# Loads that write all 128 partitions at once in place of loads that write 32 partitions with four pieces each, in a fused attention and mixture-of-experts kernel

## The chip, the cores and the metric

The kernel runs on one core of one Trainium2 chip. The metric is the device time of one execution in microseconds (us), as the median of several runs. A core has five engines, each with its own in-order instruction queue: TensorE (PE, matrix multiplies), VectorE (DVE), ScalarE (ACT), GpSimd (POOL) and SyncE (SP, which here does nothing but issue DMAs). The DMAs are executed by 16 DMA engines, which all queues share. The on-chip memory SBUF has 128 partitions; DRAM is the off-chip memory.

## The reference

Four batches of 512 tokens (width 512) go through two layers, all in float32:

```
h = layernorm(x)
q = feature_map(h @ Wq.T);  gate = sigmoid(h @ Wg.T + bg)
k, v = split(ctx @ Wkv.T);  k = feature_map(k)          # 1024 context rows, 16 heads of 32
attn = (q @ (k.T @ v)) / (q @ sum(k))                    # linear attention
x = x + (attn * gate) @ Wo.T
h2 = layernorm(x)
w, sel = top_2(h2 @ Wr);  w = softmax(w)                 # 2 of 8 experts per token
x = x + sum over the 2 experts e of w_e * (h2 @ We[e] + be[e])
```

## The kernel before, in words

**The order of the work.** PE executes its matmuls in an order written out by hand. Per batch there are eight steps over the context, `kv_tiles` (line 374; per step the products `pk` and `pv` of one 128-row tile `cT`, and `kvs`), then the query and gate projections `pq` and `pg`, the products `pz` and `pn`, and the output projection `po`. The context steps of the next batch are laid between the stages of the present one: steps 0 to 3 ahead of `po`, steps 4 to 7 behind it.

**Routing and experts.** After `po`, the router (`choose`, line 526) makes the transposes `pt`, the logits `ps` and `pl`, and the top two; `dispatch` (line 580) counts places with small matmuls `pp` and writes each token's normalized row twice, by indirect DMA from the POOL queue, into `stream`, a DRAM buffer with a region for each expert. A row is 514 floats: 512 of the token and two numbers. The buffer is first filled with empty rows (`stream<-empty`, 1 MB each, from SP). The expert tiles of 128 rows are then run by `run` (line 738): 17 early tiles of the first three batches' tokens, whose loads begin once the third batch is counted, and 18 late tiles, whose list is known only after the last batch's `dispatch`. For each tile:

- `rows` (line 742) loads the tile from `stream` into `xg` with four DMAs of 64 KB, and two numbers a row into `of`. It runs five tiles ahead of the matmuls, on five buffers.
- `turned` (line 776) transposes 32x32 blocks on DVE, three tiles ahead of the matmuls.
- `expert` (line 796) multiplies with the weights `we_sb` of the tile's expert (`pe`), and DVE adds the bias into `y`.
- POOL writes `y` by indirect DMA to `result`, a DRAM buffer with two rows a token. Later the rows are fetched back (`fetch`, line 871), added with their gates (`add`, line 896) and stored (`store`, line 911), in part between the late tiles and in part at the end.

**A layout of the weights.** A DVE transpose turns 32x32 blocks, so a token's 512 features lie in SBUF with feature 128 i + 32 c + f at partition 32 i + f of chunk c. The weights that multiply such operands, `wq`, `wg` and the eight experts' `we`, are loaded in the same layout: `load_rows` (line 132) for `wg_in` and `wq_sb` (lines 167, 173), and the loop in `kv_tiles` (line 382) for `we_sb`. Each does it with four DMAs of 256 KB; DMA i writes the 32 partitions 32 i to 32 i + 31, with four pieces of 2 KB for each. The loads `xg` do it in the same way, with four pieces of 512 bytes for each of 32 partitions. The query blocks `blocks` (`load_blocks`, line 112) are loaded with 32 partitions and sixteen pieces each.

**What sets the order around the change.** SP's queue is in order, and all of these loads are on it: first `wkv`, three `cT` tiles and four `x` tiles, then `wg_in`, `cT` tile 3, `wq_sb`, `blocks`, `wr_in`, `cT` tile 4, and the loads of `wo` and `bg`. A `cT` tile has three buffers, so that tile s + 2 is loaded when tile s - 1 has been used. The experts' weights are loaded in the second and third batches, one expert at every second context step, behind that step's `cT` load and ahead of its `stream<-empty`. SP's and ACT's DMAs share eight semaphores in turn, and each DMA waits for the one eight places before it to land. Matmuls of SP-loaded tiles wait for the semaphore of the load. DVE's, ACT's and POOL's orders are chosen by a list scheduler when the program is built.

Of the kernel before, what the change touches and what calls it, by code (L numbers as in the profile page):

```python
# [17 lines left out]
P = 128  # L18
B, L, S, D = 4, 512, 1024, 512
E, F = 8, 512  # L20
HD = 32
NC = D // P
# [31 lines left out]
def xattn_moe_kernel(  # L54
# [47 lines left out]
    def load(dst, src):  # L102
        latest["load"] = nc.sync.dma_start(out=dst, in_=src)  # L103
        tc.keep_in_program_order(latest["load"])

    def load_ctx(b, s):
        t = cpool.tile([P, ROW], F32, tag="cT", name=f"cT_{b}_{s}")
        t = t[:, 0:D].rearrange("p (c n) -> p c n", n=P)
        load(t, cT[b, s])
        return t  # L110
# [21 lines left out]
    def load_rows(dst, w):  # L132


        for i in range(NC):
            load(dst[ts(i, HD)], w.rearrange("(c f) i n -> i f c n", f=HD)[i])

    wkv_sb = wpool.tile([P, NC, 2 * D], F32, tag="wkv", name="wkv_sb")
    wq_sb = wpool.tile([P, NC, D], F32, tag="wq", name="wq_sb")
# [3 lines left out]
    nc.gpsimd.memset(wr_sb, 0.0)  # L143
    bg_sb = wpool.tile([P, NC], F32, name="bg_sb")
    we_sb = wpool.tile([P, E, NC, F], F32, name="we_sb")
    we_rows = we.rearrange("e (c f) i n -> e i f c n", f=HD)

    ctx_tiles = {}

# [172 lines left out]
    def keys(b, s):  # L322
        k = kvpool.tile([P, D], F32, tag="k", name=f"k_{b}_{s}")
        feature_map(k, half_tile(ctx_tiles[b, s], 0, "pk"))
        return k
# [27 lines left out]
    def set_empty(b, e):  # L353
        r = e * CAP + b * L
        n = L if b < B - 1 else CAP - b * L
        set_rows(r, n)
        if (b, e) == (B - 1, E - 1):
            set_rows(SLOTS, P)
            load(
                result[NOWHERE:, :].rearrange("(r p) f -> p r f", p=P),  # L360
                empty[:, 0:F].rearrange("p (o f) -> p o f", o=1).to_broadcast([P, 2 * NT, F]),
            )
# [11 lines left out]
    def kv_tiles(b, lo, hi, between=None, inside=None):  # L374
        for s in range(lo, hi):
            nxt = (b, s + 2) if s + 2 < NS else (b + 1, s + 2 - NS)
            if nxt[0] < B and nxt not in loaded_ctx:
                loaded_ctx.add(nxt)
                ctx_tiles[nxt] = load_ctx(*nxt)
            if b in (1, 2) and s % 2 == 0:  # L380
                e = (b - 1) * E // 2 + s // 2
                for i in range(NC):
                    load(we_sb[ts(i, HD), e], we_rows[e, i])
            for e in (s,) if b else (2 * (s - NS // 2), 2 * (s - NS // 2) + 1):
                if e >= 0:
                    set_empty(b, e)
            if s == 0:
                sums[b] = pkv.tile([P, NC, 2 * P], F32, tag="kvs", name="kvs")
            k = made.pop(s) if s in made else keys(b, s)
            if (b, s) == (0, 0):  # L390
                made[1] = keys(0, 1)
            if inside is not None and s == lo:
                inside()
            v = values(b, s)
            if s > 0:
                kv_add(sums[b], s - 1, *pending[b])
            pending[b] = k, v
            if between is not None:
                between(s - lo)
        if hi == NS:  # L400
            kv_add(sums[b], NS - 1, *pending[b])
# [336 lines left out]
    def run(lists, lo, n, early):  # L738
        why = "clamped to the tiles of the streams and to the experts where it is computed"
        no_i, row_i, ranked = lists  # L740

        def rows(j):


            row = nc.values_load(
                row_i[0:1, j : j + 1], [ET.SP], min_val=0, max_val=SLOTS,
                skip_runtime_bounds_check_because=why,
            )
            if (j if early else j + EARLY) % 5 < 3:
                xg = cpool.tile([P, ROW], F32, tag="cT", name="xg")  # L750
            else:
                xg = kvpool.tile([P, ROW], F32, tag="v", name="xg", bufs=2)
            of = small.tile([P, 2], F32, tag="of", name="of", bufs=8)
            rows_of = stream[ds(row, P), :]
            parts = []
            for i in range(NC):
                parts.append(
                    (
                        xg[ts(i, HD), 0:D].rearrange("t (j f) -> t j f", j=NC),
                        rows_of[:, ts(i, P)].rearrange("(j t) f -> t j f", t=HD),  # L760
                    )
                )
            parts.append((of, rows_of[:, D:ROW]))
            for dst, src in parts:
                load = nc.sync.dma_start(out=dst, in_=src)  # L765
                latest["load"] = load
                if early:
                    behind(load, written["stream"][: 2 * NT * (B - 1)], "tokens of the tile")
                    early_loads.append(load)
                    for put in scatters.get(B - 1, []):  # L770
                        tc.declare_no_dep(load.ins, put.ins, reason=full_already)
                else:
                    behind(load, written["stream"], "tokens of the tile")
            return xg, of

        def turned(j, xg, of):

            if early:
                xT = turned_rows[:, j % 4]
            else:  # L780
                xT = work.tile([P, NC, P], F32, tag="qT", name="xgT", bufs=NC)
            latest["turn"] = nc.vector.transpose(  # L782
                xT.rearrange("p c (j t) -> p j c t", t=HD),
                xg[:, 0:D].rearrange("p (j c f) -> p j c f", j=NC, f=HD),
            )

            home_i = small.tile([P, 1], U32, tag="to", name="to", bufs=8)
            tc.keep_in_program_order(latest["turn"])
            latest["turn"] = nc.vector.tensor_scalar(
                home_i, of[:, 1:2], ranked[:, j : j + 1], of[:, 0:1],  # L790
                ALU.is_equal, ALU.add,
            )
            tc.keep_in_program_order(latest["turn"])
            return xT, home_i

        def expert(j, xT, home_i):
            no = nc.values_load(
                no_i[0:1, j : j + 1], [ET.PE, ET.DVE], min_val=0, max_val=E - 1,
                skip_runtime_bounds_check_because=why,
            )  # L800
            pe = pmm.tile([P, F], F32, tag="mm", name="pe")
            for c in range(NC):
                matmul(
                    out=pe,
                    lhsT=xT[:, c, :],
                    rhs=we_sb[:, ds(no, 1), c, :].rearrange("p o f -> p (o f)"),
                    start=(c == 0),
                    stop=(c == NC - 1),
                )
            if early or j % 5 < 3:  # L810
                y = kvpool.tile([P, F], F32, tag="k", name="y")
            else:
                y = work.tile([P, F], F32, tag="ex", name="y")
            latest["y"] = nc.vector.tensor_tensor(  # L814
                y, pe, be_sb[:, ds(no, 1), :].rearrange("p o f -> p (o f)"), ALU.add
            )
            mark()
            put = nc.gpsimd.indirect_dma_start(  # L818
                out=result,
                out_offset=bass.IndirectOffsetOnAxis(ap=home_i, axis=0),  # L820
                in_=y,
                in_offset=None,
                bounds_check=2 * TOK - 1,
                oob_is_err=False,
            )
            apart(put, "result", "each choice has a row")
            for got in read_back:
                tc.declare_no_dep(put.ins, got.ins, reason=read_again)
            tc.keep_in_program_order(put)


        loaded, ready = [], []
        if early:
            turned_rows = big.tile([P, 4, NC, P], F32, tag="xT", name="turned_rows")

        def after(what):
            return tc.issue_after(latest[what].ins) if what in latest else nullcontext()

        for j in range(lo - 5, n):
            if j + 5 < n:  # L840
                with after("load"):
                    loaded.append(rows(j + 5))
            if j >= lo:
                with after("turn"):
                    expert(j, *ready.pop(0))
            if j + 3 >= lo and loaded:
                with after("y"):
                    ready.append(turned(j + 3, *loaded.pop(0)))
            yield
# [6 lines left out]
    rows_of = {}  # L856
# [96 lines left out]
    def between(i):  # L953
        for t in {1: (0, 1), 2: (2,), 3: (3,)}.get(i, ()):
            normalized_T(xT, t, blocks, ln)
# [205 lines left out]
```

## Time and profile before

| | before |
|---|---|
| median of 3 runs | 608.56 us (607.83 to 609.25) |
| the profiled execution: its time | 610.59 us |
| its span in the trace | 608.9 us |
| PE busy | 576.7 us (95%) |
| DVE / ACT / POOL busy | 289.6 / 109.3 / 120.5 us |
| PE's waits for `cT` | 6.4 us, 2 times |
| DVE's idle time that ended with an `xg` landing | 24.4 us, 12 times |
| packets of the SP and ACT queues' DMAs | 70,560, 85.15 MB |
| packets of POOL's DMAs | 8,336, 24.29 MB |

The profile is of one execution, which took 2.0 us longer than the median run. A busy row is the time in which an engine executed something; a busy PE may still be waiting in parts, as matmul ends are modelled. In the digit rows each digit is a slice of 15.2 us, in tenths. The chain of waits is followed from the last instruction back to what released each step; the engine "SPq" in it is time in which SP's queue was issuing DMAs, and "DMA xg<-stream" is the time from the issue of such a load to its landing. The DMA share is the mean busy share of the 16 DMA engines; it can come out a little over 1.

### The profile page before, as it was taken

Reading aid. Unit: us, or ns where it says so; the run is one execution under the profiler, and the core shown is the slowest. Engines: PE = TensorE matmul, PEld = TensorE weight load, DVE = VectorE, ACT = ScalarE, POOL = GpSimd, SP = SyncE. Lnnn points to the kernel's source line nnn. Section 1 sums busy time; section 2 is a strip of 40 time slices with the busy share of each in tenths; the row PEclk is TensorE's granted clock in tenths of the full one; section 3 lists DMA queues with packets and bytes.
Section 4 is the critical chain, followed back from the end, with each engine's and each line's share of the span. In section 5 each row is a group of like instructions: output and inputs, shape, how many; then the busy total and the mean of one; then the engine's idle time right before and its main releaser. Section 6 shows DMA issues by size and latency. Waiting matters only on the chain.

```text
span 608.9 us, 6440 instructions
## 1 busy us (share of the span) xinstructions
PE 576.7 (95%) x1780; PEld 270.0 (44%) x1780; DVE 289.6 (48%) x732; ACT 109.3 (18%) x168; POOL 120.5 (20%) x289
## 2 busy tenths in 40 slices
PE   7989999999999999999999999999999999998950
PEld 3545544454555435445543454554344443443420
DVE  2215254354317443541564355128765579473863
ACT  1311241220313321122242121221300110000000
POOL 4230021000001510000061100003211237444630
PEclk9989999999999999999999999999999999999995
DMA  8979995374490698627338660952255444889866
GB/s 283 166 122 355 340 197 48 116 238 131 121 277 19 140 240 261 190 87 209 103 140 147 236 203 5 315 221 108 89 119 121 121 122 167 251 235 295 243 225 212
DMA packets 78933, 109.87 MB, mean 180 GB/s; under 512 B 13229, under 2 KB 39853, under 8 KB 78768
## 3 DMA queue, kind: packets, MB, share of 16 engines
q1 hardware_dynamic: 68112, 79.91, 49.0%
q0 software_dynamic: 8336, 24.29, 12.2%
q10 hardware_dynamic: 2448, 5.24, 2.6%
q8 instruction: 15, 0.25, 0.2%
q14 instruction: 22, 0.18, 0.1%
HBM read 50.19 MB, written 59.96 MB: 181 GB/s over the span
## 4 chain that ended last, share of the span: by engine, by line
PE 74%; DMA 9%; DVE 6%; SPq 4%; issue 4%; POOL 1%; DVEq 0%; ACTq 0%; POOLq 0%
PE pk L94 18%; PE pv L94 16%; PE pq L94 9%; PE po L94 9%; PE pg L94 7%; PE pe L94 5%; PE kvs L94 4%; DMA xg<-stream 4%; DMA cT<-in_cT_dram 3%; SPq L765 2%; SPq L103 1%; PE pn L94 1%; PE pt L97 1%; DMA result<-y,to 1%; DMA of<-stream 1%
## 5 line engine op out<-in xcount | busy, mean ns | idle before, releaser
L94 PE MATMUL pk<-wkv_sb,cT 128*128 128x512 f32 x256 | 119.4, 611 | 6.4 <-DMA cT<-in_cT_dram 6.4
L94 PE MATMUL pv<-wkv_sb,cT 128*128 128x512 f32 x256 | 115.2, 593 | 0.0
L250 DVE TENSOR_SCALAR ex<-pk 128x512 f32<-128x512 f32 x32 | 22.1, 692 | 135.1 <-PE pk L94 135.1
L94 PEld LDWEIGHTS pv<-wkv_sb,cT 128*128 128x128 f32 x256 | 48.4, 190 | 62.3 <-issue 59.8
L94 PEld LDWEIGHTS pk<-wkv_sb,cT 128*128 128x128 f32 x256 | 48.0, 196 | 60.9 <-issue 53.4
L94 PE MATMUL pe<-we_sb,xgT 128*128 x144 | 62.8, 594 | 3.9 <-DVE xgT L782 3.9
L94 PE MATMUL pe<-we_sb,turned_rows 128*128 x136 | 60.4, 596 | 1.9 <-DVE turned_rows L782 1.5
L94 PE MATMUL pg<-xT,wg_sb 128*128 128x512 f32 x128 | 56.7, 595 | 0.0
L94 PE MATMUL pq<-xT,wq_sb 128*128 128x512 f32 x128 | 56.6, 596 | 0.0
L94 PE MATMUL po<-wo_sb,aT 128*128 128x512 f32 x128 | 55.6, 592 | 0.0
L818 POOL DMA_INDIRECT result<-y,to x35 | 36.4, 1041 | 94.0 <-DVE y L814 91.3
L251 ACT ACTIVATE ex<-ex 128x512 f32<-128x512 f32 x48 | 30.2, 629 | 137.5 <-DVE ex L250 117.3
L330 POOL MEMSET v<- 128x4 f32 x32 | 3.3, 108 | 245.4 <-PE kvs L94 245.3
L94 PEld LDWEIGHTS pe<-we_sb,xgT 128*128 128x128 f32 x144 | 27.1, 190 | 39.4 <-issue 32.2
L624 POOL DMA_INDIRECT stream<-rows,slot x32 | 32.9, 1027 | 51.7 <-DVE acc L587 22.2
L94 PEld LDWEIGHTS kvs<-v,k 128*128 128x128 f32 x256 | 33.3, 191 | 16.0 <-issue 14.2
L94 PEld LDWEIGHTS pe<-we_sb,turned_rows 128*128 128x128 f32 x136 | 25.2, 190 | 34.0 <-issue 29.9
L94 PEld LDWEIGHTS pg<-xT,wg_sb 128*128 128x128 f32 x128 | 24.0, 190 | 32.1 <-issue 32.1
L94 PEld LDWEIGHTS po<-wo_sb,aT 128*128 128x128 f32 x128 | 24.1, 190 | 29.2 <-issue 28.7
L94 PEld LDWEIGHTS pq<-xT,wq_sb 128*128 128x128 f32 x128 | 23.8, 190 | 27.3 <-issue 27.3
L94 PE MATMUL kvs<-v,k 128*128 128x129 f32 x256 | 34.1, 275 | 0.0
L252 DVE SCALAR_TENSOR_TENSOR k<-pk,ex 128x512 f32<-128x512 f32 x32 | 22.1, 691 | 21.6 <-ACT ex L251 21.6
(183 smaller groups left out, 459.7 us busy)
## 6 DMA issues: line engine op xcount, KB each, us to landing
stream<-empty SPq DMA_DIRECT2D x24, 1028.0 KB
stream<-empty SPq DMA_DIRECT2D x8, 1285.0 KB
xg<-stream SPq DMA_DIRECT2D x140, 64.0 KB
we_sb<-in_we_dram SPq DMA_DIRECT2D x32, 256.0 KB
cT<-in_cT_dram SPq DMA_DIRECT2D x31, 256.0 KB
y<-result POOLq DMA_DIRECT2D x10, 512.0 KB
x<-in_x_dram SPq DMA_DIRECT2D x16, 256.0 KB
blocks<-in_x_dram SPq DMA_DIRECT2D x16, 256.0 KB
```

What stands on the lines that cost most here:

```text
L94: tc.keep_in_program_order(nc.tensor.matmul(**operands))
L97: tc.keep_in_program_order(nc.tensor.transpose(dst, src, ident))
L103: latest["load"] = nc.sync.dma_start(out=dst, in_=src)
L250: nc.vector.tensor_scalar(ex, src, 0.0, None, ALU.min)
L251: nc.scalar.activation(ex, ex, AF.Exp)
L252: latest["map"] = nc.vector.scalar_tensor_tensor(dst, src, 0.0, ex, ALU.max, ALU.add)
L330: nc.gpsimd.memset(v[:, :, P : P + 1], 1.0)
L624: put = nc.gpsimd.indirect_dma_start(out=stream, out_offset=bass.IndirectOffsetOnAxis(ap=slots[i][:, t, :], axis=0), in_=rows[t], in_offse ...
L765: load = nc.sync.dma_start(out=dst, in_=src)
L818: put = nc.gpsimd.indirect_dma_start(out=result, out_offset=bass.IndirectOffsetOnAxis(ap=home_i, axis=0), in_=y, in_offset=None, bounds_ch ...
```

## The change

The three places that load with 32 partitions and four pieces are cut the other way. `load_rows` now issues one DMA for each chunk c: it writes all 128 partitions with one piece of 2 KB each. The same function serves the experts' weights in `kv_tiles`, in place of the loop. The load of an `xg` tile issues one DMA for each block of 32 tokens j: all 128 partitions, one piece of 512 bytes each. What lies where in SBUF afterwards is the same, the number of DMAs (four), the bytes of each (256 KB or 64 KB) and the size of the pieces (2 KB or 512 bytes) too.

On the DRAM side the order of the pieces changes. Before, the source of a DMA was walked as 32 rows by 4 pieces, as was the destination. Now the source is walked as 4 by 32 (`f i n -> i f n` and `t (i f) -> i t f`: the column block i is outermost, of size 4), and the destination as 128 partitions. So in the built program a `we_sb` load had the sizes 32, 4, 512 on both sides; it now has 4, 32, 512 at the source and 128, 1, 512 at the destination.

```diff
     def load_rows(dst, w):
-        for i in range(NC):
-            load(dst[ts(i, HD)], w.rearrange("(c f) i n -> i f c n", f=HD)[i])
+        for c in range(NC):
+            load(dst[:, c, :], w[ts(c, HD)].rearrange("f i n -> i f n"))
...
-    we_rows = we.rearrange("e (c f) i n -> e i f c n", f=HD)
...
                 e = (b - 1) * E // 2 + s // 2
-                for i in range(NC):
-                    load(we_sb[ts(i, HD), e], we_rows[e, i])
+                load_rows(we_sb[:, e], we[e])
...
-            for i in range(NC):
+            for j in range(P // HD):
                 parts.append(
                     (
-                        xg[ts(i, HD), 0:D].rearrange("t (j f) -> t j f", j=NC),
-                        rows_of[:, ts(i, P)].rearrange("(j t) f -> t j f", t=HD),
+                        xg[:, ts(j, P)],
+                        rows_of[ts(j, HD), 0:D].rearrange("t (i f) -> i t f", i=NC),
                     )
                 )
```

In the built program PE's order and SP's order of DMAs are the same as before. The scheduler has moved a few things on the other engines. In the second and third batches DVE makes the layernorm statistics of the next batch's `x` ahead of the copy of the router's logits (`lg`), where they stood behind it, and ACT takes the square root of these statistics ahead of the copy `share<-ps`, which the matmul `pl` needs. POOL writes and reads back the spread moments of the next batch ahead of the scatter `stream<-rows`, where they stood behind it.

## Prediction

> **What bounds the kernel now.** I read the page first, for who is busy and when the DMA engines are.
>
> ```profile
> span 608.9 us, 6440 instructions
> ...
> PE 576.7 (95%) x1780; PEld 270.0 (44%) x1780; DVE 289.6 (48%) x732; ACT 109.3 (18%) x168; POOL 120.5 (20%) x289
> ...
> PE   7989999999999999999999999999999999998950
> ...
> DMA  8979995374490698627338660952255444889866
> ...
> PE 74%; DMA 9%; DVE 6%; SPq 4%; issue 4%; POOL 1%; DVEq 0%; ACTq 0%; POOLq 0%
> ```
>
> PE is busy in nearly every slice, so in the middle a DMA counts only if it comes later than PE can wait. The DMA engines are full in the first 85 us and in the last 95 us. There the next view looks closer: busy time in chosen stretches (columns: stretch, length, five engines, granted clock, DMA share, GB/s).
>
> ```profile
> 6.00:13.00 7.00, 7.00 (x14) 2.92 (x13) 1.59 (x5) 0.63 (x1) 2.43 (x23) 1.00 1.04 342
> 15.00:23.00 8.00, 8.00 (x26) 4.03 (x25) 3.10 (x10) 2.92 (x5) 3.38 (x3) 1.00 1.03 220
> ...
> 514.00:578.00 64.00, 60.34 (x140) 26.35 (x140) 38.79 (x72) 0.00 (x0) 32.37 (x77) 1.00 0.85 250
> ```
>
> From 6 to 13 us the loads write 128 partitions (`wkv`, `cT`, `x`); from 15 to 23 us they are mostly `wg_in` and `wq_sb`, 32 partitions each. Both stretches fill the DMA engines, but move 342 and 220 GB/s. Third, the order on SP (start, length), and fourth the chain of waits near the start.
>
> ```profile
> 9.81 2.33 SPq L103 DMA_DIRECT2D wg_in<-in_wg_dram  x4
> 17.24 0.35 SPq L103 DMA_DIRECT2D cT<-in_cT_dram  x1
> 17.63 1.85 SPq L103 DMA_DIRECT2D wq_sb<-in_wq_dram  x4
> 19.53 4.15 SPq L103 DMA_DIRECT2D blocks<-in_x_dram  x4
> 23.72 2.79 SPq L103 DMA_DIRECT2D wr_in<-in_wr_dram  x1
> 26.61 0.40 SPq L103 DMA_DIRECT2D cT<-in_cT_dram  x1
> ```
> ```profile
> 26.61 12.30 DMA cT<-in_cT_dram
> 38.91 0.14 issue
> 39.05 5.37 PE pk L94 x8
> ```
>
> `cT` tile 4 stands behind `wg_in`, `wq_sb` and `blocks` and lands at 38.9 us; PE waits 2 us for it. Last, the chain in the late tiles:
>
> ```profile
> 522.46 6.57 DMA xg<-stream
> ...
> 538.02 3.97 DMA xg<-stream
> ...
> 547.51 3.04 DMA xg<-stream
> ...
> 552.44 6.74 DMA xg<-stream
> ```
>
> A tile's loads are already the wait that ends last there. PE does a tile in 3.43 us (eight records, 10.50 us for three tiles in the chain), SP issues one every 2.93 us (436.86, 439.86, 442.77), and the 18 late tiles take from 514.6 to about 584 us, 3.9 us each.
>
> **What the change does to one load.** [...] The two rows above agree (220 against 342 GB/s), so a 256 KB load would fall from 262/220 = 1.19 to 262/342 = 0.77 us. [...] The ends are therefore 0.77 us (16 engines) and, at 342/16 = 21.4 GB/s an engine, 262/85.5 = 3.07 us (four). In the packet records a 2 KB packet takes 84 ns in the first stretch, 160 ns in the second; 32 packets for each of four engines at 84 ns are 2.69 us. [...]
>
> *Start.* Eight loads cost 8 x 1.19 = 9.5 us now and 21.5 to 24.6 us on the four engines: 12 to 15 us later for all that stands behind them there, and every 16-engine load needs those four. [...] `cT` tile 3, wanted at 29.1 us, lands near 25: hidden. `cT` tile 4 lands some 10 us later, and PE, which has nothing else in its order, waits: **+10 us** (5 if the moments' traffic that now slows `blocks` falls beside it, 14 at most).
>
> *Experts' weights.* Four loads an expert, 10.8 to 12.3 us on the four engines, every second context step (15.5 us). With two `stream<-empty` (1,028 KB at 342 GB/s, 3.1 us each) and two `cT` (0.8 each) that is 18.6 to 20.1 us of work in 15.5. The lead of two tiles and `po` (13.7 us without such loads) take up four steps of it. What comes late is the next batch's `x`, behind the last of them: SP issues `we_sb` at 164.65, and 165.7 + 11.5 + 3.1 + 0.8 + 3.1 + 3.1 = 187.3 us, landed at 187.9; now its last packet starts at 182.3. That would be hidden, but the scheduler has put the statistics of `x` ahead of `lg` on DVE, and their root ahead of `share<-ps` on ACT. Statistics of the last tile (0.9), table load and root (1.28 + 0.30) and the copy (0.59) put `pl` at about 191 us instead of 184. Behind the waiting ACT stand `share`, and PE's `pl`, `pq`, `pp`. I take 5 us each for two batches (0 if `x` is in time, 7 from the sum): **+10 us**. In POOL's order the scatter now stands behind the moments' return, a wait of up to 14.3 us in the trace, and delays `blocks` and the `cT` behind it on SP; `cT` tile 2, issued at 211 and wanted at 232, covers that. Without this cover it would be a few us more.
>
> *Early tiles.* An `xg` tile is four DMAs of 32 packets of 512 bytes on each of the four engines; such a packet takes 27 ns (median of 8,720 records): 4 x 32 x 27 = 3.46 us a tile, where 16 engines needed 0.9. The first tile is landed at 440.4 and PE starts at 441.9; the last of its packets comes 1.0 + 3.46 us after the issue at 436.86, landed near 441.9. **+2 us** (0 to 4). Later ones, with the 64 packets of 4,096 bytes of each result (159 ns, 0.64 us an engine), come every 4.2 us; PE wants seven in 437 to 487 us and the rest behind lists and `dispatch`: hidden.
>
> *Late tiles.* Here the four engines become the bound. Their work is 18 x 3.46 = 62.3 us of `xg`; a sixteenth of the results, fetches and stores of POOL's queue, some 2,900 packets of 4,096 bytes at 159 ns, 28.8 us; and 2.5 us of small ones: 93.6 us. Filled to 95%, 98.5 us. From 515.6 us the last `xg` lands at 614 instead of 583.9: **+30 us**. Bounds: perfectly filled, 609 (+25); at the mean packet times, waits in them, 35 and 186 ns, 80.6 + 33.7 + 2.5 = 116.8 us (+48). The tail behind it (25 us: transpose, matmul, result, fetch, store) stays. SP's issue of the new form isn't in the trace: 0.43 us as now, or 0.60 as the dearest `wo` load of 64 rows; four of them raise SP's 2.93 us to 3.6, below the four engines' 5.2: hidden in either case.
>
> Sum: 10 + 10 + 2 + 30 = 52 us. The profiled execution would go from 610.59 us (span 608.9 and 1.7 around it) to 662.6. It lies 2.0 us above the median of the runs, so the median goes from 608.56 to **660.5 us**.
>
> **The rivals.**
> [...]
> *Four engines, but the weights are hidden*: PE's wait at the start is only 2 us now, and 5 us of late `x` may find slack. Only the tiles pay, 2 + 28: 638 us.
> *The four engines jam the middle too*: 18.6 to 20.1 us of work in each 15.5 us stretch, eight such pairs of steps; if the lead doesn't take it up, 3 to 4.6 us a pair, about 30 us more: 690 us. Against it: `po`, `pq` and `pg` drain the backlog.
>
> **How the numbers follow.** My forecast 0.67, all on 16 engines 0.06, weights hidden 0.12, jam 0.15. About 0.2% (1.2 us) is what a measurement can tell from no change. Faster 0.05 (most of the 16-engine case), same 0.02, slower 0.93. Low bounds of the four terms give 608.6 + 5 + 0 + 0 + 25 = 639, high ones 608.6 + 14 + 14 + 4 + 48 = 689. The range goes from 630, below the case of hidden weights, to 695, just over the jam; left out are the 16-engine case and the tails, under 0.2.
>
> **What would show it.** Right: 2 KB packets of `wg_in` near 84 ns with a quarter of the engines at work, so a low DMA share at 15 to 25 us while `cT` tile 4 lands near 49 us; PE waiting there for `cT`, and at `pl` in two batches; late tiles coming every 5.2 us, the four engines the cause, GB/s in the late stretch below 200. Wrong: a DMA share near 1 with 340 GB/s at 15 to 23 us (16 engines), or late tiles still at 3.9 us; then my first step, the number of engines, has failed. If the start is right and the late part is not, the packets' times on few engines are.

## The result and the profile after

The changed kernel takes **669.9 us** (median of four runs, 669.2 to 679.4) beside 608.9 us for the kernel before on the same chip: ratio **1.100, 95% interval 1.098 to 1.102**. One of the four runs, 679.4, was disturbed and is left out of the ratio. The prediction said 660.5 us, range 630 to 695, slower with 0.93. The profiled execution took 669.2 us, its span 667.4, so the spans moved by 58.5 us where 52 were predicted.

The page after (busy rows, the digit rows of PE and of the DMA engines, the chain of waits by engine):

```profile
span 667.4 us, 6441 instructions
...
PE 591.9 (89%) x1780; PEld 274.3 (41%) x1780; DVE 291.9 (44%) x732; ACT 108.8 (16%) x168; POOL 119.6 (18%) x289
...
PE   7929999999979999999799999999799987878670
...
DMA  7456996263462655437146634642233446565656
...
PE 64%; DMA 13%; DVE 6%; issue 6%; SPq 6%; POOL 2%; POOLq 0%; ACT 0%; another core or an unknown queue 0%; DVEq 0%; ACTq 0%
```

PE has a hole in the third slice (33 to 50 us), small ones in the twelfth and the twentieth (near 198 and 320 us), and a worn last quarter. The DMA row is the paradox to learn from: where the kernel before showed mostly 8 and 9 at the start and the end, there are now 4 to 7 in the first four slices and 4 to 6 in the last eight, although PE and DVE wait longer for transfers. A mean over 16 engines hides that a few are full: from 15 to 23 us it is 0.47, with 4.2 packets under way in most of it. Busy time in chosen stretches (stretch, length, five engines, granted clock, DMA share, GB/s):

```profile
6.00:13.00 7.00, 7.00 (x15) 3.01 (x14) 1.59 (x5) 0.63 (x1) 2.40 (x23) 1.00 0.95 318
15.00:23.00 8.00, 8.00 (x26) 4.12 (x25) 2.81 (x9) 2.75 (x4) 1.74 (x1) 1.00 0.47 118
35.00:50.00 15.00, 2.68 (x13) 1.53 (x11) 0.47 (x1) 0.59 (x1) 2.14 (x5) 0.75 0.52 124
550.00:640.00 90.00, 67.68 (x140) 26.41 (x139) 37.94 (x70) 0.00 (x0) 30.03 (x75) 0.94 0.59 189
```

From 6 to 13 us nearly all loads are unchanged ones (`wg_in` is issued from 10.25 us on), and the row is nearly as before. From 15 to 23 us 220 GB/s have become 118. In the packet records, 4.2 packets of 2 KB are under way at a time from 16 to 18 us (before: mostly 16), and one takes 87 ns (median from 16 to 24 us; before, to 22 us, 159). So a packet is as fast as those of the loads that write 128 partitions from 6 to 13 us, before and after (84 ns). The semaphore updates in the trace fit four engines too: in the kernel before, each of the 40 weight loads raises its semaphore 16 times as it lands; in the change it raises it five times, once soon after the issue and four times as it lands. SP's order at the start (start, length of the group):

```profile
10.25 3.96 SPq L103 DMA_DIRECT2D wg_in<-in_wg_dram  x4
16.96 0.34 SPq L103 DMA_DIRECT2D cT<-in_cT_dram  x1
17.35 11.08 SPq L103 DMA_DIRECT2D wq_sb<-in_wq_dram  x4
28.47 12.62 SPq L103 DMA_DIRECT2D blocks<-in_x_dram  x4
41.14 2.26 SPq L103 DMA_DIRECT2D wr_in<-in_wr_dram  x1
43.50 0.38 SPq L103 DMA_DIRECT2D cT<-in_cT_dram  x1
```

The four `wq_sb` loads keep SP for 11.08 us (before 1.85), `blocks` for 12.62 (4.15). The issuing itself takes up the time: `cT` tile 4 is issued at 43.50, not 26.61. The chain of waits goes on from there, and later shows the place where the second batch's routing begins:

```profile
43.50 7.30 DMA cT<-in_cT_dram
50.80 0.14 issue
50.93 6.25 PE pk L94 x8
```
```profile
186.45 11.21 DMA x<-in_x_dram
...
200.68 0.30 ACT rstd L260
200.98 0.48 ACT share L550
201.46 0.04 issue
201.50 1.88 PE pl L94 x8
203.38 8.48 PE pq L94 x16
```

PE's 2 us wait for `cT` is now 13.25. In the second piece `x` lands at 197.7, its statistics stand ahead of `share`, and `pl` starts at 201.5 in place of 184.1. The last stage is read from SP's order again (late tiles, one `xg` line each), and from the waits between 550 and 640 us (who, for what: us in total, times, longest):

```profile
600.68 3.71 SPq L763 DMA_DIRECT2D xg<-stream  x4
604.59 0.65 SPq L763 DMA_DIRECT2D of<-stream  x1
606.01 4.00 SPq L763 DMA_DIRECT2D xg<-stream  x4
610.22 0.38 SPq L763 DMA_DIRECT2D of<-stream  x1
611.38 3.73 SPq L763 DMA_DIRECT2D xg<-stream  x4
```
```profile
DVE xgT L780 <- DMA xg<-stream: 50.5, 17, 7.4
```

A tile every 5.3 us here, and nearly every tile waits for its landing. To place the loss I compare the same instruction in both traces: the first `pq` of each batch, the last batch's first `pp`, the last `xgT`, the end.

| start of | before | after | moved | gained since the row above |
|---|---|---|---|---|
| `pq`, batch 1 | 73.0 | 85.7 | +12.7 | start: 12.7 |
| `pq`, batch 2 | 184.7 | 203.2 | +18.5 | experts' weights: 5.8 |
| `pq`, batch 3 | 297.2 | 322.9 | +25.7 | experts' weights: 7.2 |
| `pq`, batch 4 | 409.7 | 436.8 | +27.1 | 1.4 |
| `pp`, batch 4 | 495.4 | 527.3 | +31.9 | early tiles: 4.8 |
| last `xgT` | 584.7 | 642.6 | +57.9 | late tiles: 26.0 |
| the end | 608.9 | 667.4 | +58.5 | tail: 0.6 |

### The profile page after: what moved, and what is told of

Read it like the earlier page. It is cut to its first block, busy times and chain, and to the rows that moved or that the text cites. A ratio compares the mean times of both kernels' runs of the same rounds, so it can differ in the third digit from the quotient of the medians.

```text
span 667.4 us, 6441 instructions
## 1 busy us (share of the span) xinstructions
PE 591.9 (89%) x1780; PEld 274.3 (41%) x1780; DVE 291.9 (44%) x732; ACT 108.8 (16%) x168; POOL 119.6 (18%) x289
## 4 chain that ended last, share of the span: by engine, by line
PE 64%; DMA 13%; DVE 6%; issue 6%; SPq 6%; POOL 2%; POOLq 0%; ACT 0%; another core or an unknown queue 0%; DVEq 0%; ACTq 0%
PE pk L94 15%; PE pv L94 14%; PE pq L94 8%; PE po L94 8%; PE pg L94 6%; PE pe L94 5%; SPq L103 4%; DMA xg<-stream 4%; DMA x<-in_x_dram 3%; PE kvs L94 3%; DMA result<-y,to 2%; SPq L763 2%; DMA cT<-in_cT_dram 2%; POOL result L816 1%; PE pn L94 1%
## 5 line engine op out<-in xcount | busy, mean ns | idle before, releaser
L94 PE MATMUL pe<-we_sb,xgT 128*128 x144 | 70.2, 635 | 22.3 <-DVE xgT L780 22.2
L94 PE MATMUL pe<-we_sb,turned_rows 128*128 x136 | 62.1, 610 | 5.7 <-DVE aT L470 3.4
L94 PE MATMUL pq<-xT,wq_sb 128*128 128x512 f32 x128 | 59.5, 621 | 0.0
L250 ACT ACTIVATE ex<-ex 128x512 f32<-128x512 f32 x48 | 30.2, 629 | 160.1 <-DVE ex L249 141.0
L94 PEld LDWEIGHTS pq<-xT,wq_sb 128*128 128x128 f32 x128 | 25.1, 201 | 29.0 <-issue 28.7
L94 PEld LDWEIGHTS po<-wo_sb,aT 128*128 128x128 f32 x128 | 24.1, 190 | 29.2 <-issue 28.7
L780 DVE STREAM_TRANSPOSE xgT<-xg 128x512 f32<-128x512 f32 x18 | 12.8, 711 | 52.5 <-DMA xg<-stream 52.5
```

Source lines behind the costliest of these rows:

```text
L94: tc.keep_in_program_order(nc.tensor.matmul(**operands))
L250: nc.scalar.activation(ex, ex, AF.Exp)
L780: latest["turn"] = nc.vector.transpose(xT.rearrange("p c (j t) -> p j c t", t=HD), xg[:, 0:D].rearrange("p (j c f) -> p j c f", j=NC, f=HD),)
```

## The experiments

The theory: a load whose source has 4 as its outermost size runs on four engines, and that is the loss. Rivals: only one of the two families of loads pays; the shape in SBUF (128 partitions, one piece each) is slow; SP's dearer issue (an `xg` load takes SP 0.557 us at the median, before 0.317); the scheduler's new order. The edits are shown shortened: the host's reordering of the weights, and the reading of a tile's row number for ScalarE's queue, are left out.

**Each family alone.** The first run keeps the new weights' loads and puts the tiles' loads back, the second the reverse.

```diff
 weights only:  - xg[:, ts(j, P)] <- rows_of[ts(j, HD), 0:D] "t (i f) -> i t f"
                + xg[ts(i, HD), 0:D] <- rows_of[:, ts(i, P)]   (as before)
 tiles only:    load_rows and we_sb as before, xg as in the change
```

> Only the weights' loads (experts', query and gate) are in the new form; the tiles of rows are loaded as before. Theory (a load whose source has 4 as its outermost count runs on four DMA engines): the start's +12.7 us and the experts' weights' +14.4 us of the traced after stay, the +4.8 and +26.6 of the tiles go: 608.9 + 27 = 636 us, 631 to 641. Rival (only the tiles pay, and what moved in the first 300 us is a shift that the later stages would have absorbed): within 2 us of 608.9. Rival (the scheduler's new order on the vector and scalar engines costs it, and the weights' loads hardly): pq of batch 2 is late by some 6 us without a late start: about 620.

> Only the tiles of rows are loaded in the new form; all weights as before. Theory: +4.8 us by the early tiles and +26.6 by the late ones: 608.9 + 31 = 640 us, 635 to 648; the sum of this run's loss and the weights-only run's is the whole loss of 61 within 5 us. If the late tiles were only late because all before them was, the time is within 10 us of 608.9.

Measured: weights only 635.5 us, ratio 1.046 (1.041 to 1.051); tiles only 639.3 us, 1.053 (1.049 to 1.057). Both families pay, 26.5 and 30.4 us; the sum of 56.9 is 4 us short of the whole. About that much is made up in the weights-only trace, which is 28.7 us late at the last batch's `pp` and 25.1 at the end: DVE takes up one of its late tiles every 3.64 us, in the kernel before every 3.88. No loss is a mere shift of an earlier one.

**The same shape in SBUF on sixteen engines.** The host lays the weights' rows in the order in which they are loaded, so that the source is 128 rows; in the second run they lie so that the load has to state 16 times 8 rows, which gives it unequal sides as in the change. Tiles are loaded as before in both.

```diff
-            load(dst[:, c, :], w[ts(c, HD)].rearrange("f i n -> i f n"))
+            load(dst[:, c, :], w[:, c, :])
 16 outermost:
+            load(dst[:, c, :], w[:, c, :].rearrange("(t u) n -> u t n", u=16))
```

> The weights are laid out in DRAM so that each load's source is 128 rows of 2 KB with 128 as its outermost count, and it writes all 128 partitions as in the change; tiles as before. Theory of the number of engines: sixteen again, so none of the 27 us is left; and as all 128 partitions are written, the loads should reach the 342 GB/s that the loads from 6 to 13 us reached, not the 220 of before's 15 to 23 us, so wq and cT are some 2 us earlier at the start: 607 us, 604 to 609.5. Rival (writing 128 partitions in one 2 KB piece each is itself what is slow, whatever the source): as the weights-only run, about 636.

> As the rows-laid run, but with the 128 source rows in an order that the load has to state as 16 times 8 rows (in place of 4 times 32 in the change), so source and destination differ in shape just as in the change and the instruction takes SP as long as in the change. Theory of the number of engines: 16 in the outermost place gives sixteen engines: within 2 us of the rows-laid run, about 607. Rival (SP's dearer issue of loads whose sides differ in shape, 0.55 us in place of 0.32, holds up SP's queue): as the weights-only run, some 636; a little over the rows-laid run (up to 3 us) if it has a small part.

Measured: 606.9 us, 0.997 (0.995 to 1.000), and 606.1 us, 0.995 (0.993 to 0.998). All 26.5 us are gone, and 2 to 3 more. An issue of `we_sb` took SP 0.597 us in the second of them and 0.430 in the first, without effect on the time. SP's order at the start of the second, to be read beside that of the change:

```profile
17.25 2.46 SPq L103 DMA_DIRECT2D wq_sb<-in_wq_dram  x4
19.75 3.40 SPq L103 DMA_DIRECT2D blocks<-in_x_dram  x4
23.20 3.31 SPq L103 DMA_DIRECT2D wr_in<-in_wr_dram  x1
26.61 0.58 SPq L103 DMA_DIRECT2D cT<-in_cT_dram  x1
```

With loads of unequal sides too, but sixteen engines, `wq_sb` takes 2.46 us of SP, not 11.08. So it is not the instruction's shape that held SP up. Nor is it the wait for the DMA eight places before: the change's longest issue, 6.73 us for the third `blocks` load, began at 32.16 us, and that earlier load had landed at 28.68. That the four engines could take no more fits all of this; how much they can hold was not measured. All 40 weight loads raise their semaphores 16 times in both runs. For the weights the theory stands; the shape in SBUF and the dearer issue are out.

**Eight engines.** The same kernel with 8 times 16 rows.

```diff
-            load(dst[:, c, :], w[:, c, :].rearrange("(t u) n -> u t n", u=16))
+            load(dst[:, c, :], w[:, c, :].rearrange("(t u) n -> u t n", u=8))
```

> As the run with 16 source rows outermost, with 8 times 16 rows in place of 16 times 8: eight engines by the theory. A 256 KB load then takes 16 packets of 85 ns on each, 1.4 us (four engines: 2.7 to 3.1). The eight loads of the start add 5.5 us over sixteen engines in place of 16.4, and cT tile 4, needed at 39 us, lands near 38; x waits for 5.4 us of weights in place of 11.6: 606 to 613 us, 609 taken. If the loss were in proportion to the engines' extra time it would be a third of the 29 us between four engines and sixteen: 616. If the number in the outermost place did not matter: 606.

Measured: 621.6 us, 1.023 (1.019 to 1.027), and 8.1 to 8.3 packets of 2 KB under way from 14 to 18 us. Each of the 40 weight loads now raises its semaphore nine times, once and then eight times. The number of engines is as expected, the time is not: I took 609. Sixteen, eight and four engines give 606, 622 and 635. PE's order in the two runs, sixteen first, shows the start's part (start, length of the group, in brackets what it waited for):

```profile
36.53 3.60 PE L94 MATMUL pk<-wkv_sb,cT 128*128 128x512 f32 x8
```
```profile
40.59 6.54 PE L94 MATMUL pk<-wkv_sb,cT 128*128 128x512 f32 x8 [3.64 <-DMA cT<-in_cT_dram]
```

`cT` tile 4 was late by 3.6 us, and the eight matmuls behind the wait took 6.54 us in place of 3.60: the start costs 7 us where I had the tile land just in time. The other 8.1 us come between there and the last `pq` (421.2 to 436.3 us, less the start's 7.0), a stretch that holds the experts' weights; it was not taken apart further.

**Why `x` is late.** The weights-only kernel, with the last of a batch's four experts' weights loaded one step sooner.

```diff
-            if b in (1, 2) and s % 2 == 0:
-                e = (b - 1) * E // 2 + s // 2
+            if b in (1, 2) and s in (0, 2, 4, 5):
+                e = (b - 1) * E // 2 + (0, 2, 4, 5).index(s)
```

> The weights-only run (635.5 us), with the last of each batch's four experts' weights loaded one step of keys and values sooner (at step 5, not 6, some 8.6 us earlier), so that x's quarter on the four engines no longer stands behind them. Theory (x of the next batch is late because the experts' weights, 11.6 us on four engines, are still ahead of it; statistics on x stand in front of the routing's work on the vector engine): most of the 7 us a batch goes, in two batches 10 to 14: 622 to 626 us. Rival (the order of instructions itself, not x's lateness, costs the 14): 635.

Measured: 623.2 us, 1.026 (1.021 to 1.032), 12 us less than weights only. DVE's wait for `x` at the end of the second batch, in the change (185 to 204 us) and then here (180 to 200 us):

```profile
DVE st L257 <- DMA x<-in_x_dram: 5.2, 1, 5.2
```
```profile
DVE st L257 <- DMA x<-in_x_dram: 1.4, 1, 1.4
```

In the weights-only run the same wait is 5.1 us. So the lateness of `x` comes from the experts' weights, which stand ahead of it on the four engines. The scheduler's order alone costs nothing that shows: the rows-laid run has the same orders on DVE, ACT and POOL as the weights-only run, instruction for instruction, and takes 606.9 us. In these runs the order cost time only where `x` was late.

**The late tiles: four engines or SP?** In the late stage of the change SP never waits for a transfer at all. These are its waits from 550 to 640 us (us in total, times, longest):

```profile
SPq L763 <- DVE y L900: 2.3, 5, 0.7
SPq L763 <- DVE y L812: 1.6, 4, 0.6
SPq L763 <- DVE to L787: 1.3, 4, 0.4
```

This speaks for SP as the bound and against a step of the prediction. For the engines speak the packet records of the same stretch: 2.83 packets of 512 bytes are under way at a time, 0.71 for each of four engines, and if all others lie evenly on sixteen, they add 0.41. That estimate of 1.12 for each of the four is as much as full engines showed at the start (16.0 packets on sixteen, before, 6 to 13 us). First run: two of a late tile's four loads from ScalarE's queue. Second run: half of each tile in the old form.

```diff
 two queues (on the tiles-only kernel):
-                load = nc.sync.dma_start(out=dst, in_=src)
+                queue = nc.scalar if not early and n_part in (1, 3) else nc.sync
+                load = queue.dma_start(out=dst, in_=src)
 half of each tile (on the tiles-only kernel):
-            for j in range(P // HD):
+            for i in range(NC):      # old form, blocks 2 and 3
+                parts.append((xg[ts(i, HD), 2 * P : D] "t (j f) -> t j f", rows_of[2 * HD :, ts(i, P)] "(j t) f -> t j f"))
+            for j in range(2):       # new form, blocks 0 and 1
```

> The tiles-only run (639.3 us), with two of the four loads of each late tile issued from ScalarE's queue, which has nothing else to do there, in place of SP's. Theory (the four DMA engines are full: 3.0 of them busy on average with the tiles' packets and 0.37 of each with scatters and fetches): who issues does not matter, 636 to 641 us. Rival (SP's issue sets the late tiles' pace: an unblocked tile takes SP 2.88 us of issue and about 1.7 more of gaps, 4.2 to 4.7 of the 5.15 us that a tile takes): with 1.5 us less on SP per tile, 20 tiles would come 30 us sooner, about 610 us.

> Of each tile of rows, blocks 0 and 1 are loaded as in the change (two loads on four engines), blocks 2 and 3 as before (four loads of 32 partitions on sixteen engines, two pieces each): six loads in place of four, and half of the work on the four engines. Theory: the tiles' packets take a busiest engine 2.2 us a tile in place of 3.6, with 1.5 us of scatters and fetches 3.7 in place of 5.1 a tile; the late tiles then just about keep pace with the rest: 609 to 617 us, 612 taken. Rival (SP's issue): six loads a tile take SP longer than the tiles-only run's four (4 x 0.32 + 2 x 0.56 + gaps of 0.19 each, about 5 us a tile with the rest): 640 us or more.

Measured: two queues 641.4 us, 1.053 (1.046 to 1.060), as tiles only; half of each tile 643.7 us, 1.060 (1.056 to 1.064), where I expected 612. Read alone, the first says "the four engines" and the second "SP". SP's waits in the late stage of the first run, and SP's order in the second:

```profile
SPq L766 <- DMA xg<-stream: 37.0, 28, 3.0
```
```profile
583.98 3.39 SPq L772 DMA_DIRECT2D xg<-stream  x6
587.57 0.35 SPq L772 DMA_DIRECT2D of<-stream  x1
588.70 3.41 SPq L772 DMA_DIRECT2D xg<-stream  x6
592.31 0.38 SPq L772 DMA_DIRECT2D of<-stream  x1
```

With two queues SP stands still for 37 us, waiting for earlier tiles' loads, and DVE still takes up a tile every 5.06 us (change 5.15, before 3.88): the engines' limit (1.15 packets for each of the four, estimated as above). With half of each tile SP issues without a pause, 4.7 us a tile and up to 5.6 with the longer issues, and waits for loads for 0.6 us in 82: SP's limit, and DVE's pace is 5.10. There are two limits of nearly one size. Relieving either brings nothing, so I relieved both.

```diff
 half of each tile, with the two four-engine loads of a late tile on ScalarE's queue:
+                queue = nc.scalar if not early and n_part in (4, 5) else nc.sync
```

> The half-of-each-tile run (643.7 us), with the two four-engine loads of each late tile issued from ScalarE's queue, so that SP issues four cheap ones and the one of two columns. Theory, amended: two limits lie close together, the four engines at 5.15 us a tile and SP's own pace of 4.2 to 4.8, and the half-of-each-tile run only went from the first to the second (4.75 us a tile there, SP never waiting). With both relieved (3.7 us a tile on the busiest engine, some 3.6 on SP), most of the late tiles' 27 us goes: 612 us, 608 to 622. Rival (neither limit; what costs is the 512-byte pieces that write 128 partitions, or the eight loads that can be under way): 635 us or more.

Measured: 627.9 us, 1.033 (1.029 to 1.038): 16 us less than with SP alone issuing, but 16 above the 612 taken, between both expectations. Part of the miss is the early tiles, which I had not moved and whose six loads a tile SP still issues: `pp` of the last batch is 6 us later than before. The rest is a pace of 4.39 us a tile, and SP again waits:

```profile
SPq L773 <- DMA xg<-stream: 17.4, 19, 2.5
```

Each load waits for the one eight places before it, and there are now seven a tile with two slow ones among them. Whether this limit or the four engines' work sets the 4.39 us stays open; the packets, at an estimated 1.09 for each of the four if all but the two new-form loads lie evenly on sixteen, speak for the engines.

**SP's issue with sixteen engines.** The kernel before, with the row's number of a late tile read into SP's register five times.

```diff
+            for again in range(1 if early else 5):
                 row = nc.values_load(row_i[0:1, j : j + 1], [ET.SP], ...)
```

> The kernel before (608.9 us, sixteen engines, all loads as they were), with SP reading the row's number of each late tile five times in place of once: four more register loads of some 0.3 us each, so that SP's unblocked tile of 3.05 us becomes about 4.3 to 4.6, which is what the change's dearer issue makes of it (4.2 to 4.7). It asks how much of the late tiles' +27 us the dearer issue would have cost if the loads had kept sixteen engines. If SP's issue is the late tiles' pace from 4.3 us a tile on, VectorE takes up a tile every 4.5 us in place of 3.88, over 18 tiles +11: 620 us, 615 to 627. If only the four engines cost anything and SP has room: 609, within 2. If SP alone explains all: 635.

Measured: 610.9 us, 1.007 (1.004 to 1.010). It does not answer the question: in its trace the four extra reads are gone, and only four semaphore instructions are left of them, 0.26 us a tile in place of the 1.2 to 1.5 meant. Eighteen times 0.26 is 4.7 us, and 4.2 were measured by the ratio (3.3 between the medians), which agrees with SP setting the pace; but DVE's pace in the profiled execution, 3.87 us, is not longer. What the dearer issue alone would cost on sixteen engines was not settled.

**Better than both.** The rows-laid kernel with two of four loads of each late tile on ScalarE's queue, and the rows-laid kernel with one load of 128 rows of 8 KB for each weight matrix.

```diff
+                queue = nc.scalar if not early and n_part in (1, 3) else nc.sync
...
-        for c in range(NC):
-            load(dst[:, c, :], w[:, c, :])
+        load(dst, w)
```

> The rows-laid run (606.9 us; weights on sixteen engines, tiles as before), with two of the four loads of each late tile issued from ScalarE's queue. If SP's issue sets the late tiles' pace in the kernel before (3.05 us a tile unblocked, 2.95 measured), the late tiles come some 0.5 us a tile sooner, but TensorE is busy for 60.3 of those 64 us, so no more than 3 us: 604. If SP has no part there: 606.9, within 1.

> The rows-laid run (606.9 us), with each weight matrix in one load of 128 rows of 8 KB in place of four of 128 rows of 2 KB: 10 loads in place of 40, sixteen engines all the same. Theory: bytes and engines are as they were, SP saves about 1.5 us an issue of four, wanted by no one: 605 to 608, no change from 606.9. Rival (SP's queue at the start, where cT tile 4 stands behind it, is still worth something): cT tile 4 is issued 1.5 us sooner, but TensorE does not wait for it any more in the rows-laid run: nothing either.

Measured: **600.8 us, 0.989 (0.985 to 0.992)**, and 605.4 us, 0.996 (0.994 to 0.998), the latter no different from 0.997 for four loads. The first is faster than any other kernel here, by more than I allowed. Its stretch of late tiles:

```profile
514.00:572.00 58.00, 58.00 (x137) 25.71 (x136) 38.43 (x72) 0.00 (x0) 30.83 (x75) 1.00 0.96 297
```

PE no longer pauses, and DVE takes up a tile every 3.31 us, 3.70 in the rows-laid run. Beyond PE's gain (the last `pe` starts 2 us earlier) the end behind it is shorter, 18.1 us in place of 21.4, so my bound of 3 us was too small. So with sixteen engines too, it mattered that SP alone issued the late tiles' loads. SP's time is the likely reason; whether a second queue also helps the transfers themselves was not tried, nor was this edit on the kernel before.

## Why the prediction was right, and where it was off

Its mechanism held: four engines for this shape, the same three places, each slower. That it would be four engines and not sixteen was the author's assumption, which no run had shown when it was made. The runs showed 4.2 packets of 2 KB under way where before had mostly 16, and five semaphore updates for each weight load in place of 16. Which four engines they are the records do not tell; that 4.2 packets were under way while several such loads were waiting says that the loads shared the same four. The start's +10 lies 2 to 5 us under the 12 to 15 that its eight loads are given; no run shows this difference, and measured were +12.7, with `blocks` keeping SP for 12.62 us in place of 4.15. The reading that spoke for a gain, 342 GB/s in the stretch of loads that write 128 partitions against 220 in that of loads that write 32, came true in the packets, 87 ns and not 159. It paid only in runs where sixteen engines stayed: in the rows-laid runs the first `pq` came 3.2 and 4.4 us earlier than before, of which 2 to 3 us are left at the end. The terms, against the profiled execution:

| step | predicted | measured |
|---|---|---|
| start | +10 | +12.7 |
| experts' weights | +10 | +14.4 up to the fourth batch |
| early tiles | +2 | +4.8 |
| late tiles | +30 | +26.6 with the tail |
| sum | +52 | +58.5 |

- **Start**: `cT` tile 4 landed at 50.8 us, predicted near 49. I had it wait behind the four engines' packets; in fact it was not even issued, because SP stood in the issue of `wq_sb` and `blocks` for 23.7 us. To PE's 11.3 us of longer wait come 0.9 us of slower matmuls behind it.
- **Experts' weights**: the chain by way of `x`, the statistics, `share` and `pl` came as told. On a scale shifted by the start's 12.7 us, `x` landed at 185.0 (187.9 in my sum) and `pl` began at 188.8, 4.7 us late where I took 5. What I had not counted is that the matmuls behind the wait were slow: eight `pl` took 1.88 us (0.79 before) and sixteen `pq` 8.48 (6.97), with the granted clock at one half from 199.5 to 206.3 us. So 5.8 and 7.2 us were lost, with 1.4 more by the fourth batch.
- **Early tiles**: the size was off by 3 us. The first `pe` is 3 us later (30.2 less 27.1), and the rest comes up to the last batch's `pp`. In the tiles-only run the same stretch lost 2.7 us, near the forecast; why it lost 2 more together with the weights was not tried.
- **Late tiles**: 5.2 us a tile was predicted, 5.15 measured, GB/s below 200 as said (189). One step failed: "SP's 2.93 us to 3.6, below the four engines' 5.2: hidden in either case". Its 0.43 "as now" is the issue of a weight load; an `xg` load took SP 0.317 us before. In the change it took 0.557 at the median and 0.687 in the mean of the late stage, so four of them add 1.0 to 1.5 us and not 0.7, and a tile costs SP 4.2 us even when nothing stands in its way. (Two small readings are off without effect: the three starts quoted for SP are 2.95 us apart, and 10.50 us for three tiles of PE are 3.50.) That the number came out right is in part luck: of two nearly equal limits, the one that I had computed was the larger.
- **The rivals**: all on sixteen engines, given 0.06, ruled out by 4.2 packets under way; weights hidden, by 26.5 us of the weights-only run; a jam in the middle, by the 14.4 us that the batches with experts' weights lost, where it needed about 30 more than the 10 predicted.

Of the 9.4 us by which the median was missed, 6.5 are these terms. The rest is where the profiled executions lay: the one of before 2.0 us above the median that I started from, the one of after 0.7 below its own.

## What to carry to other kernels

Before rearranging a load, write down the sizes that its two sides will have and look at the outermost one: with 4, an otherwise good layout got four engines here (4.2 packets under way, 635.5 us for the weights alone), and with the data laid out in DRAM so that it was 128, the same write into SBUF cost nothing (606.9 us). A low DMA share (0.47 from 15 to 23 us) together with waits for DMA was the sign of it; count the packets under way. Where an engine's issue and the transfers have nearly the same pace, relieve both before judging either, since one experiment alone would convict the wrong one.

## What the hardware showed that was not expected

- SP was not free of a load once it got to it: with four engines at work one `wq_sb` issue took 3.78 us and one 4.67, and `blocks` behind them, whose loads raise their semaphores 16 times, was held as well (12.62 us, before 4.15). With 16 rows outermost, a `wq_sb` issue took 0.54 to 0.60.
- A wait of PE cost more than its length here. These are the eight `pk` matmuls behind the wait for `cT`, before and in the change:

```profile
39.05 5.37 PE L94 MATMUL pk<-wkv_sb,cT 128*128 128x512 f32 x8 [1.99 <-DMA cT<-in_cT_dram]
```
```profile
50.93 6.25 PE L94 MATMUL pk<-wkv_sb,cT 128*128 128x512 f32 x8 [13.25 <-DMA cT<-in_cT_dram]
```

  With 8 rows outermost they took 6.54 us after a wait of 3.64, in the rows-laid run 3.70 after 0.46, and with 16 rows outermost 3.60 after none. The granted clock accounts for it: it was 1.00 over the last two groups, and 0.68 (before), 0.56 (8 outermost) and 0.59 (the change) over the others, and time multiplied by clock is 3.60 to 3.70 us in all five. The trace of before has the clock at one half from 39.6 to 43.0 us: a wait of 1.99 us was followed by 3.4 us at half clock. In the change it was at one half from 42.5 to 56.1 us, 5.2 us of them after the wait.
